# Moving a query tile and the normalisers within the second pass of a two-layer convolution kernel

## The chip, the core and the metric

The program runs on one core of one Trainium2 chip, as one launch. The metric is the device time of one execution in microseconds (us). Before the change the median of three runs is 3376.52 us (3375.67 to 3377.23).

## What is computed

The input `x` is 8 images of 384 channels by 64 x 64 pixels, float32. Two residual blocks follow each other. The first is linear attention with six heads of 64 channels, behind a group normalisation:

```python
q = apply_rope_2d(conv1x1(x, Wq, bq))
k = apply_rope_2d(conv1x1(x, Wk, bk))
v = conv1x1(x, Wv, bv)
q = jax.nn.elu(to_heads(q) * scale) + 1.0
k = jax.nn.elu(to_heads(k)) + 1.0
kv = jnp.einsum('bhnd,bhne->bhde', k, v)
k_sum = k.sum(axis=2)
normalizer = jnp.einsum('bhnd,bhd->bhn', q, k_sum)[..., None]
out = jnp.einsum('bhnd,bhde->bhne', q, kv) / (normalizer + 1e-06)
...
x = x + conv1x1(out, Wfc, bfc)
```

`kv` and `k_sum` are sums over all pixels of an image, so an image needs a first pass over its pixels for the keys and values and a second one for the queries. The second block (group normalisation, a 1x1 convolution, a filter on 8 x 8 patches in the Fourier domain, a 3x3 depthwise convolution, a gate, a 1x1 convolution) runs behind it.

## The kernel before, in words

An image is cut into eight bands of 512 pixels (`NBAND`), held as `[128, 3, 512]` tiles with channels on partitions. The images are numbered 0 to 7 here, as are the bands. The loop over images runs, for each image, the second pass of block 1 (`queries`), and then block 2 of this image woven together with the first pass of block 1 of the next image. The last image has block 2 alone behind its second pass.

The change lies in `queries` and in one helper. For each band j the second pass has four kinds of work:

- `q_project(b, j)`: three PSUM tiles `pq`, each of three matmuls in the source and six in the profile (L597). When all three are there, VectorE multiplies them by the rotary tables (L610, two instructions for each of the first two tiles and one for the third), ScalarE moves halves of the third (L624), VectorE finishes that (L625) and adds the two parts (L626). ELU plus one follows: two ScalarE passes over the whole band (L337, L338) and a VectorE instruction (L339). The result is `qc`, the query tile. The call also loads its tables `tq` by a transfer that SyncE issues.
- `q_normalise(b, j)`: 24 small matmuls into one PSUM tile `pn` (L635), then VectorE adds and takes the reciprocal (L643, L644), ScalarE and VectorE take turns to split it into bf16 parts (L648, L649, L650, L651). The result is `parts`.
- `q_spread(b, j)`: 12 small matmuls (L659) spread `parts` over the channels into four PSUM tiles `prb`, and four VectorE multiplications (L668) apply them to `qc` in place.
- `project_out(b, j)`: three PSUM tiles `pf` of six matmuls each in the profile (L676), each followed by the addition to x (L680); at the end the statistics for block 2 are gathered on ScalarE (`band_sums`, L179, L182).

`q_project` and `project_out` are generators, which yield after a PSUM tile, so that the caller can place other work between their tiles. In `project_out` there is a single yield, after the first of three. `run` takes a generator to its end.

All PSUM tiles come from one pool of eight, each one bank in size. The work tiles in SBUF that hold `qc` and its partner come from a pool of nine.

Two further generators are advanced inside the pass: `chain` (the normalisation of the next image, up to its scaled key weights) and `late` (the last band's depthwise taps and gate of the image before, ending in its contraction, L830 and L841, in images 1 to 6). In image 0 `late` is empty.

What sets the order: the source is traced in the order in which it runs, and a planner of the framework then orders the instructions of each engine by its own estimate of when each can start, the one traced earlier first where several can. On TensorE the result follows the traced order almost throughout the pass, as the timeline of the profile shows. On VectorE and ScalarE the steps of several bands are interleaved. Each engine then works through its instructions in that fixed order; semaphores hold one back until its inputs and its tile are there.

Of the kernel before, what the change touches and what calls it, by code (L numbers as in the profile page):

```python
# [16 lines left out]
CT = 3  # L17
H = W = 64
N = H * W
NBAND = 8  # L20
# [97 lines left out]
def conv_blocks_kernel(ctx: ExitStack, tc: tile.TileContext, a: dict, out: bass.AP, nb: int):  # L118
# [10 lines left out]
    def ps_tile(name):  # L129
        return psum.tile([P, 512], F32, tag="ps", name=name)  # L130

    def w_tile(shape, name):
        return work.tile(shape, F32, tag="w", name=name)
# [6 lines left out]
    def load_x(b, j):  # L140
        if b >= nb:
            return
        t = xp.tile([P, CT, BT], F32, tag="x", name=f"x_{b}_{j}")
        nc.sync.dma_start(t, x_in[b][:, :, j * BT : (j + 1) * BT])
        xt[b, j] = t
# [15 lines left out]
    def band_sums(b, layer, j, x_, out):  # L161


        n = f"{layer}_{b}"
        if j == 0:
            first = small.tile([P, CT, 6], F32, tag="first", name=f"first{n}")
            mv = small.tile([P, CT, 2], F32, tag=f"mv0{layer}", name=f"mv0_{n}")
            shift = small.tile([P, CT], F32, tag=f"shift{layer}", name=f"shift{n}")
            sums = small.tile([P, CT, 2, NBAND - 1], F32, tag=f"sums{layer}", name=f"sums{n}", bufs=2 - layer)
            for m in range(CT):  # L170
                nc.vector.bn_stats(first[:, m, :], x_[:, m, :])
                nc.vector.bn_aggr(mv[:, m, :], first[:, m, :])
            nc.vector.tensor_scalar_mul(shift, mv[:, :, 0], -1.0)
            moments[b, layer] = mv, shift, sums
            return
        mv, shift, sums = moments[b, layer]
        for m in range(CT):
            of_m = [sums[:, m, i, j - 1 : j] for i in range(2)]
            nc.scalar.activation(  # L179
                out[:, m, :], x_[:, m, :], AF.Identity, bias=shift[:, m : m + 1], accum_out=of_m[0]  # L180
            )
            nc.scalar.activation(out[:, m, :], out[:, m, :], AF.Square, accum_out=of_m[1])  # L182
# [152 lines left out]
    def elu_plus_one(x_, e):  # L335

        nc.scalar.activation(e, x_, AF.Relu, scale=-1.0)  # L337
        nc.scalar.activation(e, e, AF.Exp, scale=-1.0)  # L338
        nc.vector.scalar_tensor_tensor(x_, x_, 0.0, e, ALU.max, ALU.add)  # L339
# [250 lines left out]
    def q_project(b, j, wqs, bias, q):  # L590
        tq = qp.tile([P, 4, BT], F32, tag="turn", name=f"tq_{b}_{j}")
        nc.sync.dma_start(tq, a["tq"][:, j])
        pq = []
        for m in range(CT):
            p_ = ps_tile(f"pq_{b}_{j}_{m}")
            for t in range(CT):
                nc.tensor.matmul(  # L597
                    p_,
                    wqs[:, t, m * P : (m + 1) * P],
                    xt[b, j][:, t, :],  # L600
                    start=(t == 0),
                    stop=(t == CT - 1),
                )
            pq.append(p_)
            yield
        qc = w_tile([P, CT, BT], f"qc_{b}_{j}")
        qs = w_tile([P, CT, BT], f"qs_{b}_{j}")

        def turn(dst, src, m, table):
            nc.vector.scalar_tensor_tensor(dst, src, m, table, ALU.add, ALU.mult)  # L610

        for m in range(2):
            turn(qc[:, m, :], pq[m], bias[:, m : m + 1], tq[:, 2 * m, :])
            turn(qs[:, 1 - m, :], pq[m], bias[:, m : m + 1], tq[:, 3 - 2 * m, :])

        def by_row(ap):
            return ap.rearrange("p (r w) -> p r w", w=W)

        def columns(ap):
            return ap.unsqueeze(1).to_broadcast([P, 8, W])  # L620

        turn(by_row(qc[:, 2, :]), by_row(pq[2]), bias[:, 2:3], columns(cq2))
        for to, of in (halves, halves[::-1]):
            nc.scalar.activation(qs[to, 2, :], pq[2][of, :], AF.Identity, bias=bias[of, 2:3])  # L624
        nc.vector.tensor_mul(by_row(qs[:, 2, :]), by_row(qs[:, 2, :]), columns(sq2))  # L625
        nc.vector.tensor_add(qc, qc, qs)  # L626
        elu_plus_one(qc, qs)
        q[j] = qc
# [25 lines left out]
    def q_spread(b, j, q, rn):  # L654
        pr = [ps_tile(f"prb_{b}_{j}_{s}") for s in range(4)]
        for t in range(CT):
            for s in range(4):
                strip = slice(32 * s, 32 * s + 32)
                nc.tensor.matmul(  # L659
                    pr[s][:, t * P : (t + 1) * P],  # L660
                    expand[strip, t * P : (t + 1) * P],
                    rn[strip, :],
                    start=True,
                    stop=True,
                )
        for s in range(4):
            qq = q[:, :, s * P : (s + 1) * P]
            nc.vector.tensor_mul(qq, qq, pr[s][:, :C].rearrange("p (t n) -> p t n", t=CT))  # L668
# [3 lines left out]
    def project_out(b, j, q, mt):  # L672
        for m in range(CT):
            p_ = ps_tile(f"pf_{b}_{j}_{m}")
            for t in range(CT):
                nc.tensor.matmul(  # L676
                    p_, mt[:, t, m * P : (m + 1) * P], q[:, t, :], start=(t == 0), stop=(t == CT - 1)
                )
            xm = xt[b, j][:, m, :]
            nc.vector.scalar_tensor_tensor(xm, p_, bfc[:, m : m + 1], xm, ALU.add, ALU.add)  # L680
            if m == 0:
                yield
        if j == 1:
            differences[b] = taps_pool.tile([P, CT, BT], F32, tag="dw", name=f"differences_{b}")
        band_sums(b, 1, j, xt[b, j], differences.get(b))
# [179 lines left out]
    def layer0_chain(b, prepared):  # L865

        if b >= nb:
            return
        wk = load_weight(b, "wk", k_runs) if b else first_wk
        params = []  # L870
        if b == 0:
            sum_weight(wk, "wk")
        yield from norm_chain(b, 0, params)
        scale_weight(wk, params)
        yield
        prepared += params, wk, k_bias(b, params)
# [5 lines left out]
    def run(*chains):  # L882

        chains = list(chains)
        while chains:
            chains = [c for c in chains if next(c, chains) is not chains]
# [65 lines left out]
    def queries(b, keys, before_last, late):  # L952


        wq, qbias = keys.wq, keys.qbias
        q, done, normaliser = {}, [], {}

        def normalise(j):
            normaliser[j] = q_normalise(b, j, q[j])

        run(q_project(b, 0, wq, qbias, q))
        before_last()
        run(keys.accumulate(NBAND - 1))
        next(late, None)
        finish = keys.finish(done)
        for _ in zip(q_project(b, 1, wq, qbias, q), finish):
            pass
        prepared = []
        chain = layer0_chain(b + 1, prepared)

        next(late, None)
        if b:
            run(finish)
        normalise(0)
        run(q_project(b, 2, wq, qbias, q))
        run(finish)
        mt = done[0]
        q_spread(b, 0, q[0], normaliser.pop(0))
        project = q_project(b, 3, wq, qbias, q)
        next(project)  # L980
        normalise(1)
        run(project)
        output_ = project_out(b, 0, q.pop(0), mt)
        next(output_)
        q_spread(b, 1, q[1], normaliser.pop(1))
        normalise(2)
        run(output_)
        for j in range(2, NBAND):
            if j < NBAND - 2:
                project = q_project(b, j + 2, wq, qbias, q)  # L990
                for _ in range(2):
                    next(project)
                normalise(j + 1)
                run(project)
                next(chain, None)
            q_spread(b, j, q[j], normaliser.pop(j))
            output_ = project_out(b, j - 1, q.pop(j - 1), mt)
            if j == NBAND - 2:
                next(output_)
                normalise(j + 1)  # L1000
            run(output_)
            if j < NBAND - 2:
                next(chain, None)
            if j in (5, 7):
                load_x(b + 1, j // 6)
            next(late, None)
        run(chain)
        run(project_out(b, NBAND - 1, q.pop(NBAND - 1), mt))
        return prepared

# [87 lines left out]
    for b in range(nb):  # L1098
# [52 lines left out]
        def before_last(b=b):  # L1151
            contract(b, NBAND - 2)
# [5 lines left out]
    b = nb - 1  # L1158
# [60 lines left out]
```

## Time and profile before

| | |
|---|---|
| median of three runs | 3376.52 us (3375.67 to 3377.23) |
| profiled execution, device time | 3376.24 us |
| its span | 3374.4 us |
| TensorE matmuls busy | 3299.9 us (98%) |
| VectorE busy | 2754.2 us (82%) |
| ScalarE busy | 2006.7 us (59%) |
| mean granted TensorE clock | 0.992 of full speed |
| chain that ended last | TensorE 81%, VectorE 12%, ScalarE 4% |
| traffic | 343.35 MB, mean 102 GB/s |

In the profile PE is TensorE's matmuls, PEld its weight loads, DVE VectorE, ACT ScalarE, POOL GpSimd and SP SyncE. A line of a timeline gives the start in us from the span's beginning, the duration, the engine, the line of the kernel, the operation, what it writes and reads, shapes and count, and in brackets how long the engine stood idle before it and who ended that. A line of the view of waits gives who waited, for whom, the total in us, how often, and the longest. A line of the view by stretches gives the busy time of each engine, the granted clock, the share of the transfer engines and GB/s.

### The profile page before, as it was taken

What the parts mean: (1) busy time and instruction counts of PE and PEld (TensorE: products, weight loads), DVE (VectorE), ACT (ScalarE), POOL (GpSimd) and SP (SyncE); (2) the same over time, 40 slices, a digit from 0 to 9 for tenths busy, and PEclk for the clock granted to TensorE, in tenths of its full rate; (3) what the DMA queues carried; (4) which work ended last, traced back from release to release, by engine and by line L of the source; (5) the groups of instructions that cost most, each with busy time, mean ns of one, the idle gap of its engine ahead of it and who ended that gap; (6) DMA issues with size and microseconds to landing.
All of it is one profiled execution on the core that took longest, in us unless ns stands there. A gap on an engine that the chain in (4) does not pass through costs nothing.

```text
span 3374.4 us, 53258 instructions
## 1 busy us (share of the span) xinstructions
PE 3299.9 (98%) x21370; PEld 1851.2 (55%) x21370; DVE 2754.2 (82%) x4389; ACT 2006.7 (59%) x3911; POOL 143.1 (4%) x261
## 2 busy tenths in 40 slices
PE   8999999999999999999999999999999999999988
PEld 5544565456654566545665456654566445664454
DVE  7587788967889688896888968888688877989698
ACT  4445676556665576655665656656576565555553
POOL 0000001000010000100001000010000100000000
PEclk9999999999999999999999999999999999999999
DMA  6323235342452423534335242443333531324112
GB/s 223 111 93 108 78 98 123 104 132 61 113 124 99 134 71 90 136 101 120 85 88 136 98 120 76 112 122 104 104 95 95 140 108 53 85 70 125 57 29 48
DMA packets 151499, 343.35 MB, mean 102 GB/s; under 512 B 27364, under 2 KB 38612, under 8 KB 143060
## 3 DMA queue, kind: packets, MB, share of 16 engines
q1 hardware_dynamic: 123844, 282.85, 24.9%
q0 software_dynamic: 27216, 56.89, 11.3%
q8 instruction: 168, 2.75, 0.3%
q14 instruction: 79, 0.65, 0.1%
q10 hardware_dynamic: 192, 0.21, 0.0%
HBM read 232.70 MB, written 99.88 MB: 99 GB/s over the span
## 4 chain that ended last, share of the span: by engine, by line
PE 81%; DVE 12%; ACT 4%; issue 1%; DMA 1%; SPq 0%; DVEq 0%; ACTq 0%
PE pi L694 14%; PE pk L438 13%; PE pf L676 13%; PE pv L454 13%; PE pq L597 10%; DVE dw L797 4%; PE pw L830 4%; PE pb L729 3%; PE pd L708 2%; PE pw L841 2%; PE acc L470 2%; PE acc L483 2%; PE pn L635 1%; DVE qc L610 1%; DVE qc L339 1%
## 5 line engine op out<-in xcount | busy, mean ns | idle before, releaser
L797 DVE SCALAR_TENSOR_TENSOR dw<-ring,w_dw,dw 128x512 f32<-128x512 f32 x1401 | 978.8, 749 | 244.0 <-ACT ring L745 205.4
L438 PE MATMUL pk<-wk,x 128*128 128x384 f32 x1536 | 543.7, 495 | 0.0
L597 PE MATMUL pq<-x,wq 128*128 128x512 f32 x1152 | 528.8, 607 | 0.0
L694 PE MATMUL pi<-w_in,hf 128*128 128x384 f32 x1536 | 513.6, 491 | 1.3 <-ACT hf L332 1.3
L676 PE MATMUL pf<-qc,mt 128*128 128x512 f32 x1152 | 512.8, 598 | 0.0
L454 PE MATMUL pv<-wv,x 128*128 128x384 f32 x1344 | 470.0, 488 | 0.0
L694 PEld LDWEIGHTS pi<-w_in,hf 128*128 128x128 f32 x1536 | 288.1, 190 | 195.5 <-issue 2.7
L438 PEld LDWEIGHTS pk<-wk,x 128*128 128x128 f32 x1536 | 282.9, 190 | 204.7 <-issue 31.3
L461 ACT COPY v<-pv 128x384 f32<-128x384 f32 x224 | 108.6, 485 | 424.6 <-PE pv L454 416.6
L454 PEld LDWEIGHTS pv<-wv,x 128*128 128x128 f32 x1344 | 253.6, 190 | 181.4 <-issue 8.4
L676 PEld LDWEIGHTS pf<-qc,mt 128*128 128x128 f32 x1152 | 213.6, 190 | 253.2 <-issue 239.7
L597 PEld LDWEIGHTS pq<-x,wq 128*128 128x128 f32 x1152 | 212.8, 192 | 248.6 <-issue 235.4
L680 DVE SCALAR_TENSOR_TENSOR x<-pf,bfc,x 128x512 f32<-128x512 f32 x192 | 141.4, 745 | 109.9 <-PE pf L676 109.6
L337 ACT ACTIVATE qs<-qc 128x1536 f32<-128x1536 f32 x64 | 95.0, 1484 | 144.2 <-DVE qc L626 122.3
L830 PE MATMUL pw<-gated,w_out 128*128 128x256 f32 x768 | 179.3, 383 | 0.0
L441 DVE TENSOR_TENSOR kc<-pk,kbias 128x384 f32<-128x384 f32 x256 | 141.1, 551 | 38.3 <-PE pk L438 38.1
L179 ACT ACTIVATE differences<-x,shift 128x512 f32<-128x512 f32 x168 | 119.8, 713 | 86.2 <-DVE x L680 86.2
L701 ACT COPY ht<-pi 128x384 f32<-128x384 f32 x256 | 115.0, 482 | 91.3 <-PE pi L694 87.7
L830 PEld LDWEIGHTS pw<-gated,w_out 128*128 128x128 f32 x768 | 146.7, 192 | 36.9 <-issue 6.5
L860 POOL DMA_DIRECT2D out_dram<-y x63 | 80.7, 1281 | 1873.7 <-DVE dw L797 842.0
L337 ACT ACTIVATE ks<-kc 128x1536 f32<-128x1536 f32 x64 | 95.0, 1485 | 97.1 <-DVE kc L445 92.2
L624 ACT ACTIVATE qs<-pq,qbias 64x512 f32<-64x512 f32 x128 | 87.3, 682 | 109.4 <-DVE qc L610 108.4
(177 smaller groups left out, 4459.8 us busy)
## 6 DMA issues: line engine op xcount, KB each, us to landing
tq<-in_tq SPq DMA_DIRECT2D x64, 1024.0 KB, 4.8
x<-in_x SPq DMA_DIRECT2D x64, 768.0 KB, 6.0
tk<-in_tk SPq DMA_DIRECT2D x64, 768.0 KB, 4.3
out_dram<-x SPq DMA_DIRECT2D x63, 768.0 KB, 3.3
out_dram<-y POOLq DMA_DIRECT2D x63, 768.0 KB, 7.8
xs<-in_x SPq DMA_DIRECT2D x56, 768.0 KB, 5.8
dw<-tap POOLq DMA_DIRECT2D x14, 512.0 KB, 4.8
wk<-in_wk SPq DMA_DIRECT2D x8, 576.0 KB, 3.8
```

The source lines that it names most:

```text
L179: nc.scalar.activation(out[:, m, :], x_[:, m, :], AF.Identity, bias=shift[:, m : m + 1], accum_out=of_m[0])
L337: nc.scalar.activation(e, x_, AF.Relu, scale=-1.0)
L438: nc.tensor.matmul(pk[:, :C], tokens(t), wks[:, t, :], start=(t == 0), stop=(t == CT - 1))
L441: nc.vector.tensor_add(kc[:, i, :], pk[:, :C], bias)
L454: nc.tensor.matmul(pv[:, :C], xt[b, j][:, t, i * P : (i + 1) * P], wvs[:, t, :], start=(t == 0), stop=(t == CT - 1),)
L597: nc.tensor.matmul(p_, wqs[:, t, m * P : (m + 1) * P], xt[b, j][:, t, :], start=(t == 0), stop=(t == CT - 1),)
L676: nc.tensor.matmul(p_, mt[:, t, m * P : (m + 1) * P], q[:, t, :], start=(t == 0), stop=(t == CT - 1))
L680: nc.vector.scalar_tensor_tensor(xm, p_, bfc[:, m : m + 1], xm, ALU.add, ALU.add)
L694: nc.tensor.matmul(p_[:, :C], h[:, t, i * P : (i + 1) * P], w_in[:, t, :], start=(t == 0), stop=(t == CT - 1),)
L701: nc.scalar.copy(ht[:, i, :], p_[:, :C])
L797: nc.vector.scalar_tensor_tensor(acc[:, m], src, wd, acc[:, m], ALU.mult, ALU.add)
L830: nc.tensor.matmul(p_[h][:, m - m0, :], w_out[:, 0, m * P : (m + 1) * P], gated[:, h * HT : (h + 1) * HT], start=(m == m0), stop=False,)
```

## The change

In `project_out` the generator now yields after the first and the second of its three tiles. In `queries` the order of the steps changes; no computation is added or left out.

- The first tile of band 3's queries is projected ahead of band 0's spread, where it stood behind it.
- In the loop over j = 2 to 5, band j+2's queries are projected in one go, and normaliser j+1, which stood between the second and third tile of that projection, follows band j's spread.
- For j = 6, normaliser 7 stands behind the second tile of band 5's projection to x, where it stood behind the first.
- For j = 7, the last spread stands behind the first tile of band 6's projection to x, where it stood ahead of it.

```diff
@@ project_out
             nc.vector.scalar_tensor_tensor(xm, p_, bfc[:, m : m + 1], xm, ALU.add, ALU.add)
-            if m == 0:
+            if m < CT - 1:
                 yield
@@ queries
         mt = done[0]
-        q_spread(b, 0, q[0], normaliser.pop(0))
         project = q_project(b, 3, wq, qbias, q)
         next(project)
+        q_spread(b, 0, q[0], normaliser.pop(0))
         normalise(1)
         run(project)
         output_ = project_out(b, 0, q.pop(0), mt)
...
         for j in range(2, NBAND):
             if j < NBAND - 2:
-                project = q_project(b, j + 2, wq, qbias, q)
-                for _ in range(2):
-                    next(project)
-                normalise(j + 1)
-                run(project)
+                run(q_project(b, j + 2, wq, qbias, q))
                 next(chain, None)
+            output_ = project_out(b, j - 1, q.pop(j - 1), mt)
+            if j == NBAND - 1:
+                next(output_)
             q_spread(b, j, q[j], normaliser.pop(j))
-            output_ = project_out(b, j - 1, q.pop(j - 1), mt)
             if j == NBAND - 2:
                 next(output_)
+                next(output_)
+            if j < NBAND - 1:
                 normalise(j + 1)
             run(output_)
```

## The prediction

> **What bounds the kernel now.** I read the page first. TensorE is busy for nearly the whole span and VectorE for four fifths, so time can only be won where TensorE stands still.
>
> ```profile
> span 3374.4 us, 53258 instructions
> ...
> PE 3299.9 (98%) x21370; PEld 1851.2 (55%) x21370; DVE 2754.2 (82%) x4389; ACT 2006.7 (59%) x3911; POOL 143.1 (4%) x261
> ```
>
> Next the view of waits, TensorE alone. Two of its rows belong to the function that is changed: the spread of the normaliser waits for `parts`, and the normaliser's matmuls wait for the last step of a query tile. Each happens seven times, in images 1 to 7 of 0 to 7.
>
> ```profile
> engine line waited for: us in total, times, longest us
> PE prb L659 <- DVE parts L651: 17.0, 7, 2.4
> PE pb L729 <- DVE tf L716: 14.2, 6, 3.6
> PE pn L635 <- DVE qc L339: 10.5, 7, 1.6
> ```
>
> Then TensorE's timeline of one second pass (image 4). Only the first spread waits; pq is a query tile (three of six matmuls), pn a normaliser, prb a spread, pf a projection to x.
>
> ```profile
> 1827.74 7.99 PE L597 MATMUL pq<-x,wq 128*128 128x512 f32 x18
> 1838.16 0.35 PE L659 MATMUL prb<-parts,expand 32*128 32x128 bf16 x12 [2.42 <-DVE parts L651]
> 1838.44 2.84 PE L597 MATMUL pq<-x,wq 128*128 128x512 f32 x6
> 1841.21 0.86 PE L635 MATMUL pn<-qc,ks_bd 128*32 128x128 f32 x24
> 1842.00 5.42 PE L597 MATMUL pq<-x,wq 128*128 128x512 f32 x12
> 1847.26 2.74 PE L676 MATMUL pf<-qc,mt 128*128 128x512 f32 x6
> 1849.93 0.35 PE L659 MATMUL prb<-parts,expand 32*128 32x128 bf16 x12
> 1850.20 0.86 PE L635 MATMUL pn<-qc,ks_bd 128*32 128x128 f32 x24
> ```
>
> The other wait, near the end of the pass (image 3), before the eighth normaliser:
>
> ```profile
> 1517.31 2.84 PE L676 MATMUL pf<-qc,mt 128*128 128x512 f32 x6
> 1521.72 0.86 PE L635 MATMUL pn<-qc,ks_bd 128*32 128x128 f32 x24 [1.57 <-DVE qc L339]
> 1522.52 5.42 PE L676 MATMUL pf<-qc,mt 128*128 128x512 f32 x12
> ```
>
> Last the granted clock in the 4 us behind the first wait, images 3 and 4 (the third number from the right; before it stand the busy times of the five engines): after the same gap it is low in one and full in the other.
>
> ```profile
> 1425.90:1429.90 4.00, 3.98 (x18) 1.53 (x18) 3.89 (x8) 1.36 (x2) 0.00 (x0) 0.69 0.60 182
> 1838.10:1842.10 4.00, 3.94 (x43) 1.92 (x43) 3.89 (x9) 1.36 (x2) 0.00 (x0) 1.00 0.56 195
> ```
>
> The same stretch shows 0.57, 0.62 and 0.67 in images 1, 2, 5 and 1.00 in 6 and 7. So four of seven first waits are followed by a slow clock. Its price: from first to second spread it is 13.40 us in image 3 (1425.92 to 1439.32) and 11.77 in image 4 (1838.16 to 1849.93), 1.63 more; four times, 6.5 us.
>
> All sums below are against the profiled execution, 3376.24 us (span 3374.4 and 1.84 around it); the median of the runs is 0.28 higher.
>
> **Part 1: a query tile ahead of the first spread.** No instruction is added. Six matmuls (2.77 us, 1838.44 to 1841.21) move in front of prb(0). They need x and wq, long there, and one of the eight PSUM tiles of the pool (banks below). The `parts` of tile 0 end 0.06 us before prb(0) starts, held by VectorE and ScalarE and not by TensorE, so they stay where they are. Cover 2.77 against a wait of 2.43: the wait goes, 0.34 to spare. Gross gain 17.0 us, and the 6.5 us of slow clock.
>
> What is late next? TensorE now reaches the second spread earlier: in image 4 at 1835.74 (start of the wait) + 2.77 + 0.28 (prb) + 0.79 (pn) + 5.26 (pq) + 2.67 (pf) = 1847.51. VectorE has hardly a gap in between:
>
> ```profile
> 1841.54 0.55 DVE L668 TENSOR_TENSOR qc<-qc,prb 128x384 f32<-128x384 f32 x1
> 1842.00 1.75 DVE L626 TENSOR_TENSOR qc<-qc,qs 128x1536 f32<-128x1536 f32 x1
> 1843.67 0.29 DVE L643 TENSOR_SCALAR rn<-pn 128x128 f32<-128x128 f32 x1
> ...
> 1846.89 1.76 DVE L339 SCALAR_TENSOR_TENSOR qc<-qc,qs 128x1536 f32<-128x1536 f32 x1 [0.18 <-ACT qs L338]
> 1848.56 0.34 DVE L649 SCALAR_TENSOR_TENSOR rn<-part,take_off,rn 128x128 f32<-128x128 bf16 x1
> 1848.83 0.74 DVE L610 SCALAR_TENSOR_TENSOR qs<-pq,qbias,tq 128x512 f32<-128x512 f32 x1
> 1849.49 0.34 DVE L651 SCALAR_TENSOR_TENSOR parts<-part,take_off,rn 128x128 bf16<-128x128 bf16 x1
> ```
>
> Two things gate TensorE there: `parts` of tile 1 (L651, ends 1849.83 now) and, for pn(2) right behind it, the end of query tile 2 (L339, ends 1848.65). The latter hangs on L626 and two ScalarE passes of 1.5 us and on nothing that the change moves forward. So pn(2), at 1850.20 now, can start at 1848.7 at best (1.5 us won) and at 1850.2 at worst (nothing won, the first wait has just moved). Between these I go by the nearest row, normaliser 0: there L651 ends 0.26 us after L339. With pn(1) now done 2.5 us sooner (its L643 can precede L626, as normaliser 0's does: 1830.22 and 1830.42) I take L651 at 1848.9, prb(1) 0.3, pn(2) at 1849.25: 0.95 us won in an undisturbed pass. The wait that is left there, some 1.4 us, is like those of 1.57 us before pn(7), behind none of which the clock fell, so in the other four passes the clock is won too: 16.11 us from wait to pn(2) in image 3 (1423.49 to 1439.60) becomes 13.51, 2.60 won. Together 3 x 0.95 + 4 x 2.60 = 13.2 us; ends 0 (wait and clock as now, at the second spread) and 23.5 (17.0 + 6.5).
>
> The multiplications of spread 0 (L668) start up to 2.7 us later; pf(0) waits for them, and they ended 5.17 us ahead of it (1842.09, 1847.26). The new pf(0) comes at 1844.84, which leaves up to 2.7. Banks: at prb(1) three pq, one pf and four prb make eight, as now; pn(2) needs that VectorE has read a pq by then (two L610, 1.3 us), inside the interval above.
>
> **Part 2: normalisers 3 to 6 behind their spread.** Twenty-four matmuls (0.79 us) move behind the third pq (2.77) and a spread (0.28), four instructions of VectorE (0.29 + 0.95 + 0.35 + 0.34) and two casts of ScalarE (0.3 each) behind four multiplications (0.55 each); they queue on VectorE ahead of the additions to x (L680), which release pf banks that are not wanted for another 8 us. No DMA is issued by the moved steps, so SP and POOL keep their order; the table loads of the query tiles are issued with the tiles as before. Cover: `parts` 3 to 5 lie 15.8 to 17.5 us ahead of their spread in the images read; 3 less changes nothing. Normaliser 6 is the tight one: 5.2 us from pn to `parts`, and 7.93 (a projection) are left before its spread. Without that cover it would cost 5.2 us a pass. Cost 0; ends 0 and 1 us a pass.
>
> **Part 3: another projection tile ahead of normaliser 7.** Six matmuls (2.67 us) stand in front of pn(7), whose wait is 1.57 (1.14 in the last image). They need the multiplications of tile 5, done 5.5 us before. The cover is larger by 1.1 us, and normaliser 6's four VectorE instructions (1.93) may come into the chain of tile 7. Gain 10.5 us if the wait goes; if all 1.93 falls on the chain, 0.83 remains in each pass (1.57 + 1.93 - 2.67) and some 5 us are won. I take 10.5: tile 7's own steps are traced earlier than normaliser 6.
>
> **Part 4: last spread behind a projection tile.** pn(7) and prb(7) both move by one tile, so the 9.4 us between them stay (5.3 in the last image, where `parts` takes 3.9). The last projection needs the multiplications of tile 7, 5.8 us early now (5.4 in the last image), 2.7 less afterwards. Cost 0.
>
> **Sum.** 13.2 + 10.5 = 23.7 us: 3376.24 - 23.7 = 3352.5, with the median's offset 3353. Image 0 has neither wait and stays.
>
> **A rule against the row.** The Trainium skill, TensorE: Matmul & The Clock Gate (HAM oscillation), says that idle gaps beyond about 3.4 us cost the clock. The gaps here are 2.4 us, and the clock fell after four of seven: the measurement differs, and decides. By the page the slow clock would not hang on this wait, and the sum would be smaller by what the clock gives.
>
> **Rivals.** *The first wait only moves.* VectorE keeps its order and `parts` 1 ends at 1849.83 as now: the second spread waits 2.4 us, the clock falls as often. Only part 3 is won: 3366. For it: VectorE is busy for 103.78 of the 112 us from 1409 to 1521. Against: `parts` 1 has its matmuls sooner. *Everything is won*: tile 2 gets ready sooner too, 34 us, 3342. Against: the L339 chain above.
> *The banks become the bound, slower.* Behind prb(j) now come pn and pf at once, with three pq, four prb and pn holding all eight banks. If pf must take a bank of prb, it waits for VectorE's current instruction (1.75), a first multiplication (0.55), less the 0.79 of pn: 1.5 us, at four places in eight passes 48 us, so 3376 + 48 - 24 = 3400. It outweighs the gain from 0.74 us a place on. Against: the first pq is read 5.6 us before pf needs a bank in a middle tile (1467.4, 1473.0), though only 1.9 for the tile before (1452.83, 1454.73).
> *The change does nothing*: the planner could order TensorE as before; its order follows the traced one throughout the pass, so this is faint, 3376.
>
> **How the numbers follow.** Forecast 0.58 (3343 to 3360), the wait only moves 0.18 (3360 to 3371), everything won 0.07, banks or another new wait 0.12, nothing 0.05. About 0.2% (6.8 us) can be told from no change. The first three are faster but for a small part of the second: faster 0.82, same 0.06, slower 0.12. The range leaves out the slower cases and half of the nothing: from 3342, everything won, to 3371, where only the lower end of part 3 is left.
>
> **What would show it.** Right: no wait of TensorE at prb(0) or pn(7), clock 1.00 behind prb(0), a wait of 1 to 1.5 us at prb(1) or pn(2), L643 of tile 1 earlier against L626, pn(j+1) directly behind prb(j). Wrong: 2.4 us at prb(1) with a slow clock behind it, a wait of pf for L668 or L610 in tiles 2 to 5, a spread 6 that waits for `parts`, or VectorE instructions of late depthwise taps (L797) put ahead of L339 or L651.

## The result and the profile after

The change makes the kernel slower: 3406.40 us, median of five runs (3402.58 to 3407.89), against 3376.52; the ratio is 1.0085, 95% interval 1.0073 to 1.0096. The forecast was 3353. The execution that was profiled took 3402.58 us, the lowest of the five, and its span is 3400.8. So the two traces hold 26.3 of the 29.9 us that the medians are apart.

The page of the kernel after, the same lines as before: TensorE is busy a little longer (3303.5 for 3299.9) in a span that is 26.4 longer.

```profile
span 3400.8 us, 53243 instructions
...
PE 3303.5 (97%) x21370; PEld 1856.2 (55%) x21370; DVE 2754.7 (81%) x4389; ACT 2001.4 (59%) x3911; POOL 143.2 (4%) x261
```

TensorE's waits after (who waited, for whom, total in us, times, longest):

```profile
PE prb L659 <- DVE parts L651: 37.4, 16, 3.2
PE pb L729 <- DVE tf L716: 14.2, 6, 3.6
PE ps_r L281 <- DVE rsg L310: 12.8, 14, 2.4
...
PE pf L676 <- DVE qc L668: 3.4, 7, 0.5
```

The row of L281 before:

```profile
PE ps_r L281 <- DVE rsg L310: 4.8, 7, 2.4
```

The wait of `pn` for L339 (10.5 us before) is gone. Waits of a spread for `parts` have grown by 20.4 (17.0 to 37.4), waits in the next image's normalisation (L281) by 8.0 (4.8 to 12.8), and 3.4 at a projection are new; 1.3 more are at another step of that normalisation. Less the 10.5 that are gone, that is 22.6 us more waiting, and with 3.6 us more of busy time 26.2 of the 26.4.

TensorE's timeline of image 3 after shows the places:

```profile
1433.23 0.35 PE L659 MATMUL prb<-parts,expand 32*128 32x128 bf16 x12
1433.51 0.86 PE L635 MATMUL pn<-qc,ks_bd 128*32 128x128 f32 x24
1434.30 5.42 PE L597 MATMUL pq<-x,wq 128*128 128x512 f32 x12
1440.20 2.84 PE L676 MATMUL pf<-qc,mt 128*128 128x512 f32 x6 [0.48 <-DVE qc L668]
1444.88 0.35 PE L659 MATMUL prb<-parts,expand 32*128 32x128 bf16 x12 [1.84 <-DVE parts L651]
...
1495.68 0.57 PE L281 MATMUL ps_r<-rsg,of_group 32*128 32x1 f32 x4 [1.31 <-DVE rsg L310]
...
1515.14 7.99 PE L676 MATMUL pf<-qc,mt 128*128 128x512 f32 x18
1526.23 0.51 PE L659 MATMUL prb<-parts,expand 32*128 32x128 bf16 x12 [3.10 <-DVE parts L651]
1526.67 8.20 PE L676 MATMUL pf<-qc,mt 128*128 128x512 f32 x12
1534.80 0.86 PE L635 MATMUL pn<-qc,ks_bd 128*32 128x128 f32 x24
```

The first spread and pn(7) no longer wait. But 0.48 + 1.84 us of wait stand at the projection and the second spread, where 2.43 stood at the first, and spread 6 waits 3.10. In the kernel before, the same spread of image 3 did not wait:

```profile
1517.04 0.34 PE L659 MATMUL prb<-parts,expand 32*128 32x128 bf16 x12
```

The wait of spread 6 appears in all eight images (2.75 to 3.2). Behind it twelve matmuls take 8.20 us that take 5.42 elsewhere. The view by stretches has the granted clock (third number from the right) at half:

```profile
1525.50:1532.30 6.80, 6.07 (x19) 2.76 (x20) 2.73 (x7) 2.58 (x8) 0.00 (x0) 0.50 0.25 98
```

Between 200 and 3180 us the clock was at half for 13.7 us in the trace before, and for 30.7 in the trace after.

### The profile page after: what moved, and what is told of

Read it like the earlier page. It is cut to its first block, busy times and chain, and to the rows that moved or that the text cites. A ratio compares the mean times of both kernels' runs of the same rounds, so it can differ in the third digit from the quotient of the medians.

```text
span 3400.8 us, 53243 instructions
## 1 busy us (share of the span) xinstructions
PE 3303.5 (97%) x21370; PEld 1856.2 (55%) x21370; DVE 2754.7 (81%) x4389; ACT 2001.4 (59%) x3911; POOL 143.2 (4%) x261
## 3 DMA queue, kind: packets, MB, share of 16 engines
q8 instruction: 168, 2.75, 0.3%
## 4 chain that ended last, share of the span: by engine, by line
PE 79%; DVE 14%; ACT 4%; issue 2%; DMA 1%; SPq 0%; DVEq 0%; ACTq 0%
PE pi L694 14%; PE pk L438 13%; PE pf L676 13%; PE pv L454 12%; PE pq L597 8%; DVE dw L797 4%; PE pw L830 4%; PE pb L729 3%; PE pd L708 2%; PE pw L841 2%; PE acc L470 2%; PE acc L483 2%; DVE qc L610 2%; DVE qc L626 1%; PE pn L635 1%
## 5 line engine op out<-in xcount | busy, mean ns | idle before, releaser
L676 PE MATMUL pf<-qc,mt 128*128 128x512 f32 x1152 | 531.2, 614 | 3.4 <-DVE qc L668 3.4
L597 PE MATMUL pq<-x,wq 128*128 128x512 f32 x1152 | 512.0, 597 | 0.0
L624 ACT ACTIVATE qs<-pq,qbias 64x512 f32<-64x512 f32 x128 | 87.4, 683 | 198.8 <-DVE qc L610 198.0
L337 ACT ACTIVATE qs<-qc 128x1536 f32<-128x1536 f32 x64 | 95.0, 1484 | 159.3 <-DVE qc L626 159.1
L337 ACT ACTIVATE ks<-kc 128x1536 f32<-128x1536 f32 x64 | 95.0, 1485 | 98.1 <-DVE kc L445 93.3
```

The lines of the kernel that those rows point to most:

```text
L597: nc.tensor.matmul(p_, wqs[:, t, m * P : (m + 1) * P], xt[b, j][:, t, :], start=(t == 0), stop=(t == CT - 1),)
L676: nc.tensor.matmul(p_, mt[:, t, m * P : (m + 1) * P], q[:, t, :], start=(t == 0), stop=(t == CT - 1))
```

## Why spread 6 waits: the place of one short instruction

`parts` of tile 6 come 5.2 us behind their matmuls in the kernel before, and 10.96 after. VectorE's timeline, image 3 before:

```profile
1506.20 0.29 DVE L643 TENSOR_SCALAR rn<-pn 128x128 f32<-128x128 f32 x1
...
1507.06 0.94 DVE L644 RECIPROCAL rn<-rn 128x128 f32<-128x128 f32 x1
...
1508.49 0.35 DVE L649 SCALAR_TENSOR_TENSOR rn<-part,take_off,rn 128x128 f32<-128x128 bf16 x1
...
1511.00 0.35 DVE L651 SCALAR_TENSOR_TENSOR parts<-part,take_off,rn 128x128 bf16<-128x128 bf16 x1
...
1511.83 0.69 DVE L625 TENSOR_TENSOR qs<-qs,sq 128x512 f32<-128x512 f32 x1
```

The normaliser is through before query tile 7 gets to its step L625. After the change:

```profile
1516.70 0.68 DVE L625 TENSOR_TENSOR qs<-qs,sq 128x512 f32<-128x512 f32 x1
1517.31 0.28 DVE L643 TENSOR_SCALAR rn<-pn 128x128 f32<-128x128 f32 x1
1517.51 1.75 DVE L626 TENSOR_TENSOR qc<-qc,qs 128x1536 f32<-128x1536 f32 x1
1519.17 0.94 DVE L644 RECIPROCAL rn<-rn 128x128 f32<-128x128 f32 x1
1520.03 1.31 DVE L680 SCALAR_TENSOR_TENSOR x<-pf,bfc,x 128x512 f32<-128x512 f32 x2
1521.27 0.34 DVE L649 SCALAR_TENSOR_TENSOR rn<-part,take_off,rn 128x128 f32<-128x128 bf16 x1
...
1524.16 1.75 DVE L339 SCALAR_TENSOR_TENSOR qc<-qc,qs 128x1536 f32<-128x1536 f32 x1
1525.83 0.34 DVE L651 SCALAR_TENSOR_TENSOR parts<-part,take_off,rn 128x128 bf16<-128x128 bf16 x1
```

and ScalarE beside it:

```profile
1519.35 1.48 ACT L337 ACTIVATE qs<-qc 128x1536 f32<-128x1536 f32 x1 [2.69 <-DVE qc L626]
1520.74 0.28 ACT L648 CAST part<-rn 128x128 bf16<-128x128 f32 x1
1521.04 1.28 ACT L338 ACT_TABLE_LOAD   x1
1522.33 1.48 ACT L338 ACTIVATE qs<-qs 128x1536 f32<-128x1536 f32 x1
1523.72 0.28 ACT L650 CAST part<-rn 128x128 bf16<-128x128 f32 x1
```

The normaliser's steps of 0.3 to 0.9 us now alternate with those of query tile 7: L644 behind L626 (1.75), L648 behind L337 (1.48), L650 behind a table load and L338 (1.28 + 1.48), L651 behind the scaling of query weights and L339. Normalisers 3 to 5 fare alike in that image (12.2, 12.7 and 10.3 us for 3.7, 3.8 and 3.9), but a query tile and a projection, some 16 us, lie ahead of their spread. Ahead of spread 6 there is only the projection, 7.93.

## The experiments

| kernel | median, us | ratio to before | 95% interval |
|---|---|---|---|
| the change | 3406.40 | 1.0085 | 1.0073 to 1.0096 |
| first move alone | 3376.44 | 0.9999 | 0.9990 to 1.0008 |
| normalisers 3 to 6 alone | 3431.98 | 1.0161 | 1.0144 to 1.0178 |
| last two moves alone | 3364.51 | 0.9963 | 0.9950 to 0.9976 |
| change, normaliser 6 back | 3364.43 | 0.9962 | 0.9951 to 0.9974 |
| change, spread 6 later | 3366.78 | 0.9971 | 0.9959 to 0.9982 |
| change, normaliser 6 ahead of spread 5 | 3361.55 | 0.9952 | 0.9937 to 0.9967 |
| change, ELU passes of tile 7 left out | 3363.64 | 0.9960 | 0.9945 to 0.9975 |
| change, normalisers 3 to 6 ahead of the spread | 3361.12 | 0.9954 | 0.9937 to 0.9970 |
| first move with normaliser 1 ahead of spread 0 | 3379.37 | 1.0010 | 1.0001 to 1.0020 |
| fold behind band 2's queries, alone | 3360.94 | 0.9954 | 0.9940 to 0.9969 |
| last two moves, and the fold | 3348.66 | 0.9914 | 0.9899 to 0.9928 |

### One part of the change at a time

First move alone:

```diff
-        q_spread(b, 0, q[0], normaliser.pop(0))
         project = q_project(b, 3, wq, qbias, q)
         next(project)
+        q_spread(b, 0, q[0], normaliser.pop(0))
```

> Only the first move is made: band 3's first query tile ahead of the first spread. Theory (the first wait only moves): no wait at the first spread, some 2.3 us in its place at the second spread and the projection ahead of it, in images 1 to 7, as the trace of the change shows (0.48 and 1.84); the wait before normaliser 7 (1.57) stays. 7 x (2.32 - 2.43) = -1 us, and up to 6.5 us less where the slow clock goes: 3369 to 3377. Rival (the prediction's part 1, most of the wait is won): 3363. Rival (this move is what makes the kernel slower): 3390 or more.

3376.44: nothing won and nothing lost. Over the images the waits at a spread sum to 13.2 us and those at the projection to 3.4, where 17.0 stood at the spread; the slow clock stands at 13.7 us as before, now behind the second spread (1435.1 in image 3, where that spread waits 1.83 from 1432.42). The wait has moved, clock and all.

Normalisers alone:

```diff
-                project = q_project(b, j + 2, wq, qbias, q)
-                for _ in range(2):
-                    next(project)
-                normalise(j + 1)
-                run(project)
+                run(q_project(b, j + 2, wq, qbias, q))
                 next(chain, None)
             q_spread(b, j, q[j], normaliser.pop(j))
             output_ = project_out(b, j - 1, q.pop(j - 1), mt)
             if j == NBAND - 2:
                 next(output_)
+            if j < NBAND - 1:
                 normalise(j + 1)
```

> Only normalisers 3 to 6 are moved behind their spread. Theory (normaliser 6 comes so late that its steps on VectorE and ScalarE stand between those of query tile 7): spread 6 waits some 3 us in all eight images, the parts come 10 to 11 us after their matmuls where it was 5.2, the slow clock follows in most images (1.7 us each), the wait before normaliser 7 goes because TensorE is late there, and some 1.3 us of wait per image arise at the next image's normalisation (L281): 3376 + 25 + 8 + 14 - 10 = 3413, 3399 without the slow clock. Rival (spread 6 waits only because the other moves bring TensorE there sooner): 3376.

3431.98, 55.6 more than before and 19 more than my theory gave. The direction is that of the theory and the rival falls, but the sizes were too small: spread 6 waits 3.99 us, L281 1.98, and the clock is at half for 81.9 us between 200 and 3180 (13.7 before).

```profile
1544.53 0.51 PE L659 MATMUL prb<-parts,expand 32*128 32x128 bf16 x12 [3.99 <-DVE parts L651]
```

The parts do not add up: 0, +55.6 and -11.8 make 43.8, and the whole change costs 29.9. In the whole change the same waits are shorter (3.10 and 1.31): there `parts` come 10.96 us behind their matmuls, here 11.86. Why the other moves make them come sooner stays open.

The last two moves alone (the second `yield` in `project_out`, and the lines for j = 6 and 7):

> Only the two last moves are made: a second projection tile ahead of normaliser 7, and the last spread behind a projection tile. Theory: the wait before normaliser 7 goes, nothing takes its place, 10.5 us: 3366. Rival (tile 7 is ready later by as much, or the last spread or projection waits): 3376 or more.

3364.51, as expected. The wait before normaliser 7 is gone, and the wait at the first spread is as it was (17.0 us).

### The sixth normaliser

```diff
-                run(q_project(b, j + 2, wq, qbias, q))
+                project = q_project(b, j + 2, wq, qbias, q)
+                if j == 5:
+                    for _ in range(2):
+                        next(project)
+                    normalise(j + 1)
+                run(project)
...
-            if j < NBAND - 1:
+            if j < NBAND - 1 and j != 5:
                 normalise(j + 1)
```

> The whole change, but normaliser 6 stands again between the second and third tile of band 7's queries. Theory: the wait at spread 6 goes (8 x 3.1 = 24.5 us) and the slow clock behind it (some 8 x 1.7 = 13.5), everything else as with the change, the 1.3 us at L281 too: 3406 - 38 = 3368. Rival (the wait comes from the other moves, or another takes its place): 3395 to 3406.

3364.43: with one of four normalisers put back, the change is a gain. No wait is left at spread 6; those at the second spread and at L281 (13.2 and 13.1 us in all) remain. So the wait at spread 6 causes the loss. The next run gives it more cover: for j = 6 the first projection tile stands ahead of the spread.

```diff
-            if j == NBAND - 1:
+            if j >= NBAND - 2:
                 next(output_)
             q_spread(b, j, q[j], normaliser.pop(j))
             if j == NBAND - 2:
                 next(output_)
-                next(output_)
```

> The whole change, but spread 6 stands behind the first tile of band 5's projection to x, so that 10.6 us of TensorE's work lie between normaliser 6 and its spread, not 7.93. Theory (normaliser 6 takes 11 us beside query tile 7, and TensorE merely arrives too soon): the wait at spread 6 falls from 3.1 to 0.4 us and little slow clock is left behind it: 3406 - 8 x 2.7 - 13 = 3372, 3385 if half of the slow clock stays. Rival (TensorE's delay also delays the parts, so the wait stays about 3 us): 3400 or more.

3366.78. The wait is 0.52 (0.4 expected), with `parts` 10.96 us behind their matmuls as in the change, and the clock is at half for 6.8 us in all. So TensorE's arrival does not hold the parts back; more work in between covers them.

Then the order within band 5 of the loop, normaliser 6 ahead of spread 5 but still behind all tiles of band 7's queries:

```diff
+            if j == 5:
+                normalise(j + 1)
             q_spread(b, j, q[j], normaliser.pop(j))
...
-            if j < NBAND - 1:
+            if j < NBAND - 1 and j != 5:
                 normalise(j + 1)
```

> The whole change, but normaliser 6 stands ahead of spread 5 and still behind all three tiles of band 7's queries. Theory (what counts is that its matmuls come behind the last tile of the queries, so that its steps mix with that tile's ELU): parts 10 to 11 us behind the matmuls as with the change, wait at spread 6 2.8 us (3.1 less the 0.28 of spread 5): 3403. Rival (the four multiplications of spread 5, 1.95 us, stand ahead of normaliser 6 on VectorE and make it late): wait 1 us or less: 3380.

3361.55: the theory fell, and the rival has the wait right (1 us or less; there is none). Normaliser 6 need not stand ahead of the last tile of the queries. 0.28 us of matmuls on TensorE decide over 6.4 us: `parts` come 4.55 us behind their matmuls, for 10.96. VectorE's timeline in image 3 shows how:

```profile
1500.64 0.75 DVE L610 SCALAR_TENSOR_TENSOR qc<-pq,qbias,cq 128x512 f32<-128x512 f32 x1 [0.51 <-PE pq L597]
1501.46 0.29 DVE L643 TENSOR_SCALAR rn<-pn 128x128 f32<-128x128 f32 x1
1501.79 0.95 DVE L644 RECIPROCAL rn<-rn 128x128 f32<-128x128 f32 x1
1502.65 0.50 DVE L668 TENSOR_TENSOR qc<-qc,prb 128x384 f32<-128x384 f32 x1
1503.07 0.68 DVE L625 TENSOR_TENSOR qs<-qs,sq 128x512 f32<-128x512 f32 x1
1503.66 0.34 DVE L649 SCALAR_TENSOR_TENSOR rn<-part,take_off,rn 128x128 f32<-128x128 bf16 x1
1503.92 1.75 DVE L626 TENSOR_TENSOR qc<-qc,qs 128x1536 f32<-128x1536 f32 x1
1505.59 0.35 DVE L651 SCALAR_TENSOR_TENSOR parts<-part,take_off,rn 128x128 bf16<-128x128 bf16 x1
```

Between L610 and L625 query tile 7 waits for ScalarE (L624, 1.38 us). What VectorE's order has in that gap is done at once: here the normaliser's first two steps and one of the spread's multiplications, and in the kernel with the change all four multiplications, behind which the normaliser falls between L625 and L626 and so among the ELU passes. A theory that says this was put to all four normalisers:

```diff
+            if j < NBAND - 2:
+                normalise(j + 1)
             q_spread(b, j, q[j], normaliser.pop(j))
...
-            if j < NBAND - 1:
+            if j == NBAND - 2:
                 normalise(j + 1)
```

> The whole change, but normalisers 3 to 6 all stand directly ahead of the spread that they follow in the change. Theory (the first step of a normaliser must reach VectorE while ScalarE moves halves of the query tile's third part, L624, ahead of L626; behind the spread's multiplications it misses that and stands behind L626 and both ELU passes): parts 4 to 6 us behind the matmuls in bands 3 to 6 alike, where they were 10 to 13 with the change, no wait at spread 6: 3358 to 3364. Rival (band 7 is a special case): 10 us or more in bands 3 to 5.

3361.12. In image 3 `parts` come 5.7, 4.8, 10.1 and 4.8 us behind their matmuls for normalisers 3 to 6: three of four as expected, normaliser 5 not. The trace shows that the fourth missed the gap: a step of the next image's normalisation (L281) stands ahead of its matmuls on TensorE and waits 0.99 us, so they end at 1485.36, L625 begins at 1485.41, and L643 comes at 1488.75, behind L626. In the last image, behind which no other image is normalised, normaliser 5 takes 4.8 us too. Its 10.1 us cost nothing, as a query tile and a projection lie ahead of its spread.

Last, the ELU passes. For band 7 the two ScalarE instructions L337 and L338 are left out:

```diff
-        elu_plus_one(qc, qs)
+        if j == NBAND - 1:
+            nc.vector.scalar_tensor_tensor(qc, qc, 0.0, qs, ALU.max, ALU.add)
+        else:
+            elu_plus_one(qc, qs)
```

> The whole change, with the two ScalarE passes of ELU of query tile 7 left out (its values are then not those of the reference). Theory (these two passes, the table load between them and the VectorE step behind them stand in normaliser 6's chain): parts at most 8 us behind the matmuls, no wait at spread 6, no slow clock there: 3406 - 24.5 - 13.5 = 3368. Rival (VectorE's load in that stretch, with the scaling of the query weights and the gate, makes the parts late): a wait of 2 us or more stays: 3390 or more.

3363.64. In image 3 spread 6 starts at 1511.69 with no wait, and the normaliser's last step ends at 1511.52, 7.7 us behind its matmuls (1503.83); it is so in images 1 to 7, and in image 0 1.26 of the 2.75 us of wait are left. Its L643 still stands behind the multiplications and ahead of L626. The ELU passes account for 3.3 of the 10.96 us, enough for the whole wait.

### The head of the pass

The first move with normaliser 1 ahead of spread 0:

```diff
-        q_spread(b, 0, q[0], normaliser.pop(0))
         project = q_project(b, 3, wq, qbias, q)
         next(project)
         normalise(1)
+        q_spread(b, 0, q[0], normaliser.pop(0))
```

> The first move alone, with normaliser 1 ahead of the first spread, not behind it. Theory (with the first move the multiplications of spread 0 and the first step of normaliser 1 reach VectorE behind L626 of query tile 2; swapped, normaliser 1 gets there sooner): parts 1 come 7 to 8 us behind their matmuls, where they came 10.45 with the first move, the wait at the second spread falls from 1.84 to 0.7 us or less, and query tile 2 is next: 3376.4 - 7 x 1.2 = 3368, 3361 where the slow clock goes too. Rival (VectorE's whole load at the head of the pass is the limit, whatever the order): waits of 2.3 us in all stay there, 3376.

3379.37, a little slower (1.0001 to 1.0020), where the theory gave 3368. Its first half came in direction: `parts` 1 come 9.6 us behind their matmuls in image 3, for 10.45, and the second spread waits no longer. But the multiplications of spread 0 now come later, and the projection waits for them:

```profile
1433.90 2.84 PE L676 MATMUL pf<-qc,mt 128*128 128x512 f32 x6 [1.90 <-DVE qc L668]
```

These waits sum to 13.3 us, and L281 waits 10.8 where it waited 5.0 with the first move alone: the rival's 3376 is the nearer. In both runs the shift of order at the head of the pass only moved the wait. What does help is to take work out of the way. The fold (`finish`: six matmuls and nine copies of ScalarE, 3.4 us of them in a row ahead of band 1's first ELU pass) is not needed before the first projection. It is traced behind band 2's queries:

```diff
-        if b:
-            run(finish)
         normalise(0)
         run(q_project(b, 2, wq, qbias, q))
         run(finish)
```

> The kernel before, with nothing but the fold traced behind band 2's queries in images 1 to 7. Theory (it wins by itself what it won beside the last moves, 3364.5 - 3348.7 = 15.9 us): 3360.5; the wait before normaliser 7 (1.6) stays. Rival (TensorE is held at normaliser 7 for as much as it came sooner): 3370 or more.

3360.94, as expected: waits at a spread fall from 17.0 to 3.1 us. With the last two moves added:

> The two last moves, and besides in images 1 to 7 the fold of the key-value matrix with the output weights (six matmuls, 2.1 us, and nine copies of ScalarE) is traced behind band 2's queries, where it stood ahead of normaliser 0. Theory: 2.1 us more work between normaliser 0 and its spread and 3.4 us of ScalarE copies out of the way of band 1's ELU: the first wait falls from 2.4 to 0.4 us or less and the slow clock behind it goes; as the second spread is then next, 0.9 to 2.4 us an image are won: 3364 - 6 - 6.5 = 3351, between 3345 and 3358. Rival (it only moves, as with the change's first move): 3364.

3348.66, faster than both kernels (0.9899 to 0.9928). In image 3 `parts` of tile 0 come 6.6 us behind their matmuls, for 10.3; these 3.7 us are by themselves more than the wait of 2.43, and the first spread does not wait. In each of images 1 to 7 some 0.46 us are left at the second (image 3):

```profile
1412.78 2.10 PE L508 MATMUL pm<-wfc,kvt 128*128 128x384 f32 x6
1414.81 0.34 PE L659 MATMUL prb<-parts,expand 32*128 32x128 bf16 x12
...
1427.32 0.35 PE L659 MATMUL prb<-parts,expand 32*128 32x128 bf16 x12 [0.46 <-DVE parts L651]
```

## Why the prediction was wrong, by its own steps

**Part 2 failed, and with it the sign.** It named normaliser 6 as the tight one, with 7.93 us of cover, and then set against it the 5.2 us that the kernel before shows. That latency belongs to the old place, ahead of the last query tile. At the new place the normaliser shares VectorE and ScalarE with that tile's last steps and takes 10.96: a wait of 3.10 us where the step had 0 with an upper end of 1. That is 24 us of waiting in eight images (37.4 less seven times 1.84 and 0.3 in image 0), and slow clock behind it in seven. One of the prediction's own signs of being wrong, a spread 6 that waits for `parts`, is what came, and in image 0 too, which it left as it was. The step did list the four multiplications of the spread ahead of the normaliser on VectorE; it did not carry that through to what the normaliser would then stand behind. It also did not look at the next image's normalisation, which `chain` advances at the same place: L281 waits 8.0 us more in all. This stays with normaliser 6 back (13.1 us) and is absent without the normalisers' move (4.8 and 5.0 in the runs of the last two moves and of the first alone), so it comes with normalisers 3 to 5; by which step is not shown.

**Part 1 was wrong in size.** The first wait went, and the prediction saw that the second spread would be next. But it took 0.95 us an image as won, from the pattern of normaliser 0, and 1.65 of slow clock besides in four images. The first move alone wins 0.0 (0.9990 to 1.0008). The step that failed is the claim that L643 would precede L626: with the change three of the four multiplications of spread 0 stand behind L626 (1437.00 in image 3), and L643 (1440.06) behind them. The projection, to which the prediction left up to 2.7 us, waits 0.48 for the last of them. So what came of this move is the rival "the first wait only moves", with its slow clock.

**Parts 3 and 4 were right.** 10.5 us were forecast, and the two moves, which were not run apart, give 11.8 (3376.4 to 3364.5).

**The rival on the slower side** had the right sign through another mechanism. It let `pf` wait for PSUM tiles at four bands; no such wait for L610 appears, and the 0.48 us that `pf` waits for L668 are for its input. The price that it was given (3400) is near the measured time by chance. The range, 3342 to 3371, held none of this, as it took part 2 at no more than 1 us a pass and left the chance of 12% outside.

**The slow clock.** The prediction counted it as something to win. It doubled as a price: the stretch at half clock between 200 and 3180 us grew by 17.1 us, and the busy time of the matmuls by 3.6. The sentence on the Trainium skill (TensorE: Matmul & The Clock Gate, HAM oscillation), that idle gaps beyond about 3.4 us cost the clock, differs from these runs further: gaps of 2.8 to 3.2 us at spread 6 were followed by it in images 1 to 7, all seven; the gap of 2.75 in image 0 was not.

## What to carry to other kernels

When a step moves, its latency moves with it: work out anew what it will stand behind on every in-order engine that it passes, and do not carry over the time that it took at its old place. A chain of short steps that alternates between two engines is cheap where those engines idle and dear beside long instructions, so place it in a gap that the trace shows, and check the consumer with the least cover first. Where moving a step only moves a wait, look for work that can be taken out of the stretch, as the fold was here.

## What the runs showed of the hardware that I had not expected

The granted clock fell to half behind gaps of TensorE well below 3.4 us: behind 2.43 in four of seven images, behind 0.48 and 1.84 close together in four of seven with the first move alone, and in none with normaliser 6 ahead of spread 5, where the same two gaps stand. The same gap may cost or not.

The clock's record in the traces hints at why. In the trace before, the slow stretches between 200 and 3180 us last 3.41 us each and begin at 601.42, 1014.43, 1427.44 and 2250.05, whole multiples of 3.413 us apart; in every other trace the slow stretches begin on such a grid too, at another offset. Of the seven gaps of 2.43 us before, the four that were followed by slow clock have 1.89 to 2.43 us within one interval of the grid, right ahead of the stretch; the other three are cut by its edge, with at most 1.72 us on one side. With the first move alone the same holds of the gaps of 1.84 us (1.80 or more for four, at most 1.63 for three). So where a gap falls in this grid seems to count, and the offset of the grid differs from trace to trace. No run moved a gap to test it, and it does not sort all cases: with the change, 2.01 us within one interval (image 0) had no slow clock behind them, and 1.25 (L281 in image 6) had.

Matmuls of one kind in a row are a little cheaper than broken ones: in image 3 the three PSUM tiles of a query tile with a normaliser between them took 8.89 us before (1463.18 to 1472.07) and 8.69 behind each other after, the normaliser's 0.79 included (1468.54 to 1476.44, and 0.79).
